# Input loads on ScalarE's DMA queue, and 27 in place of 23 activations turned by way of memory

## The chip, the cores and the metric

One core of one Trainium2 chip. The time is device microseconds of one execution, the median of the runs given. Lower is better.

## The reference

Sixteen batches of 256 tokens with 256 features (float32) go through two blocks, with 16 heads of 16 features. In the kernel's terms each batch passes three attentions and an MLP:

```
layer 0: cross attention on y, RMS norm before and after, residual (no mask in effect: all ones)
layer 1: layer norm, causal self attention with rotary positions, residual
layer 2: layer norm, cross attention on y with rotary positions, residual
MLP:     layer norm, fc1 (256 to 1024), GELU, fc2, residual
```

The output is 16 x 256 x 256 float32. Layers 1 and 2 and the MLP need the normalized activations turned, features on partitions and tokens along the row; layer 0 reads copies of x and y that the host laid out turned (`xt`, `yt`).

## The kernel before

The 48 attentions (16 batches, three layers) run one after the other in the hand-written order `ORDER = "000001010102210210210121021012210101021212122222"`, a layer's number for each place. `attended(j)` gives the batch of place j and the place (`below`) of the attention whose output it reads. The eight MLPs, on two batches each, come after the attentions. Instructions are issued in the program's order, which the code fixes by hand; engines wait for each other by semaphores.

One turn i of the main loop is attention i, in four blocks n (three for a causal one). In each block TensorE computes scores (S, L566), ScalarE their exponentials (pt, L577), GpSimd zeroes the causal half (pt, L584), and TensorE multiplies by the values (A, L605) one block later, the last part in the next attention. Between them stand parts of the neighbours:

- n = 0: `end` of attention i - 1 copies the second half of its result to memory (`hop<-av`, L623) and reads it back as sums and as `oT` (L630, L635); `pieces_in` of a turn that attention i - 1 hosted; `finish` and `divide` of earlier attentions; `q` of attention i + 1.
- n = 1: `k` of attention i + 1, and `invert` of attention i - 1, which takes the reciprocal of the sums on VectorE (L642) and sends it through memory (`inv_hop`, `inv`). For a causal attention `k` comes first, otherwise `invert`.
- n = last but one: `v` of attention i + 1, and `pieces_out` for a hosted turn.
- n = last: `project` of attention i - 2 (the output matmul and the residual; in layer 0 also the sums of squares and r_o, L246, for the norm), and a turn on TensorE if one is due.

Activations are turned in one of two ways. On TensorE, `turned` makes four 128 x 128 transposes with the identity (L286) and a copy on ScalarE (L296). By way of memory, `pieces_out` normalizes (xn, L271), transposes 32 x 32 blocks on VectorE (L306), and writes to memory (`turn_hop`, L311); `pieces_in` reads them back in four DMAs (`hT`, L317) one attention later. `turned_ahead` assigns each attention j of layers 1 and 2 a host m from j - 8 to j - 3 in which its `pieces_out` is issued, by matching with augmenting paths; those without a host are turned on TensorE in attention j - 2 (`due_turn`).

The tile of `pieces_out` has the tag "a", of which there are two buffers; `rotated` (the rotary part of q and k, L468) and `fold_bias` use the same tag. PSUM holds two pairs of banks for S and one for A.

Loads of weights and of later batches stand in a list `due`. When the attention three places ahead is of layer 0, four loads of 256 KB for its batch (`cur`, `y`, `xT`, `yT`) go to the front of the list. `load_next` takes from it and issues on SP's queue, which also carries every hop, turn and reciprocal.

Of the kernel before, what the change touches and what calls it, by code (L numbers as in the profile page):

```python
# [28 lines left out]
N_ATT = 3 * B  # L29

ORDER = [int(n) for n in "000001010102210210210121021012210101021212122222"]
# [15 lines left out]
def attended(j):  # L47

    b = ORDER[:j].count(ORDER[j])
    return b, [i for i in range(N_ATT) if ORDER[i] == ORDER[j] - 1][b] if ORDER[j] else None  # L50


def turned_ahead():


    slots = {}

    def place(j, tried):
        for m in range(j - 3, max(attended(j)[1] + 2, j - 8), -1):
            if ORDER[m] != 1 and m not in tried:  # L60
                tried.add(m)
                if m not in slots or place(slots[m], tried):
                    slots[m] = j
                    return True
        return False

    for j in range(N_ATT):
        if ORDER[j] > 0:
            place(j, set())
    return slots  # L70
# [3 lines left out]
def xattn_kernel(  # L74
# [21 lines left out]
    nc = tc.nc  # L96
# [580 lines left out]
    def att(i):  # L677
        if i is not None and 0 <= i < N_ATT:
            return atts.setdefault(i, Att(i))
        return None  # L680

    def do(i, *names):
        a = att(i)
        for name in names:
            if a is not None:
                getattr(a, name)()
# [287 lines left out]
    with tc.manual_schedule():  # L974
# [34 lines left out]
            due.append((fc2_sb[:, 2 * j : 2 * j + 2], fc2[j * D : (j + 1) * D]))  # L1009
        due = [(t, w.rearrange("(k p) n -> p k n", p=P)) for t, w in due]  # L1010

        def load_next(i, n, later):

            if not (i > 1 and ahead is not None and ahead.layer == 0):
                n = later if i > 2 else 0
            for t, w in due[:n]:
                nc.sync.dma_start(out=t, in_=w)
            del due[:n]

        turns = turned_ahead()  # L1020
        for i in range(N_ATT):
            a, last = att(i), att(i - 1)
            sent, due_turn = turns.get(i), i + 2 if i + 2 not in turns.values() else None
            fresh = sent is not None and att(sent).below == i - 3
            ahead = att(i + 3)
            if i > 1 and ahead is not None and ahead.layer == 0:
                due[:0] = batch(ahead.b)
            load_next(i, 2, 1)

            finishing = i >= 3 and att(i - 3).layer == 0
            follows = finishing and i + 2 < N_ATT and att(i + 2).below == i - 3
            for n in range(len(a.blocks)):
                if n == 0 and a.causal and not finishing:
                    do(due_turn, "stats")
                a.scores(n)
                if n > 0:
                    a.values(n - 1)
                elif last is not None:  # L1040
                    last.values(-1)
                final = len(a.blocks) - 1
                if n == 0:
                    if i == 0:
                        a.v()
                        do(1, "spread")
                    late = finishing and i + 2 < N_ATT and att(i + 2).layer == 0
                    if not follows and not late and (finishing or not a.causal):
                        do(due_turn, "stats")
                    if sent is not None and not fresh:  # L1050
                        do(sent, "stats")
                    do(i - 1, "end")
                    do(turns.get(i - 1), "pieces_in")
                    if late:
                        do(due_turn, "stats")
                    do(i - 3, "finish")
                    if follows:
                        do(due_turn, "stats")
                    if fresh:
                        do(sent, "stats")  # L1060
                    if not finishing:
                        do(due_turn, "norm")
                    if i == N_ATT - 3:
                        mlps[0].stats()
                    if i == N_ATT - 2:
                        mlps[0].norm()
                    do(i - 2, "divide")
                    if i == N_ATT - 1:
                        mlps[0].turn(nc.vector.tensor_copy)
                        mlps[0].keep()  # L1070
                    if i + 1 < N_ATT:
                        att(i + 1).q(both=not a.causal)
                elif n == 1:

                    if a.causal:
                        do(i + 1, "k", "second_mask")
                    if last is not None:
                        last.invert(lambda: do(i + 2, "send"))
                    else:
                        do(i + 2, "send")  # L1080
                    do(i + 2, "receive")
                    load_next(i, 1, 1)
                    if not a.causal:
                        do(i + 1, "k")
                    if finishing:
                        do(due_turn, "norm")
                    for j in kept.get(i, ()):
                        att(j).keep()
                    if i == N_ATT - 1:
                        do(i - 2, "project")  # L1090
                        mlps[1].norm()
                if n == final - 1:
                    do(i + 1, "v")
                    do(sent, "pieces_out")
                    if i == N_ATT - 2:
                        mlps[1].stats()
                    if i == N_ATT - 1:
                        mlps[0].up(2)
                        mlps[0].mix("hT", HT_LIVE)
                if n == final:  # L1100
                    if i == N_ATT - 1:
                        mlps[1].turn(nc.vector.tensor_copy)
                    else:
                        do(i - 2, "project")
                    do(due_turn, "turn")
                    load_next(i, 1, 0)
                if i == 0 and n == 0:
                    load(4)
                    nc.sync.dma_start(out=bias_sb, in_=rows.partition_broadcast(P))
                    nc.sync.dma_start(out=turn_sb, in_=turn)  # L1110
                if i == 0 and n == 1:
                    load_w(ca_sb, ca[:1], nc.sync)
                if i == 1 and n == 0:
                    load_w(sao_sb, [sa_o], nc.sync)
                if i == 1 and n == 2:
                    nc.sync.dma_start(
                        out=rope_sb, in_=rope.rearrange("(c p) t d -> p c t d", p=P)
                    )
                if i == 1 and n == 3:
                    att_hop = fold_bias(  # L1120
                        [(sa_sb, j * D, V_B1) for j in range(3)] + [(ca_sb, 0, V_B2)]
                    )
                if i == 2 and n == 2:
                    att_cols = fold_back(att_hop)
                    row_v = fc2_sb[:, 0]
                    nc.sync.dma_start(out=row_v, in_=att_hop[2].partition_broadcast(P))
                if i == 2 and n == 3:
                    fold_gain(sa_sb, slice(0, 3 * D), V_G1)
                if i == 3 and n == 3:
                    fold_att(att_cols, row_v)  # L1130
                if i == 8 and n == 2:
                    fold_gain(ca_sb, slice(0, D), V_G2)
                if i == 11 and n == 3:
                    fc1_hop = fold_bias([(fc1_sb, j * D, V_B3) for j in range(4)])
                if i == 12 and n == 1:
                    fc1_cols = fold_back(fc1_hop)
                if i == 14 and n == 2:
                    fold_fc1(fc1_cols)
                if i in (14, 15) and n == 1:
                    fold_gain(fc1_sb, slice(0, FF), V_G3, [i - 14], nc.gpsimd)  # L1140
                if n == 1 and i > 15 and not a.causal:
                    next(combined, None)
# [12 lines left out]
        for g in range(B // 2):  # L1155
            this = mlps[g]
            ahead, next_but_one, third = (
                mlps[i] if i < B // 2 else None for i in (g + 1, g + 2, g + 3)
            )
# [67 lines left out]
    with tc.If(n_good < P):  # L1227
        with tc.tile_pool(name="gen", bufs=1) as gen, tc.tile_pool(
# [4 lines left out]
                out=hop.rearrange("(n p) -> p n", p=P),  # L1233
                in_=qk_bias.rearrange("p n t -> p (n t)"),
# [3 lines left out]
                out=qk_row.rearrange("p n d -> p (n d)"), in_=hop.partition_broadcast(P)  # L1238
# [5 lines left out]
        with tc.tile_pool(name="late2", bufs=2) as late2, tc.tile_pool(  # L1244
# [3 lines left out]
            for g in range(B // 2):  # L1248
                m = Mlp(g, late2)
# [393 lines left out]
```

## Time and profile before

| What | us |
|---|---|
| median of 3 runs (lowest, highest) | 936.03 (930.95, 939.96) |
| profiled execution, its own time | 938.71 |
| span of the profile | 936.7 |
| TensorE busy | 918.8 |
| VectorE busy | 679.6 |
| ScalarE busy | 530.8 |
| GpSimd busy | 310.8 |
| attentions, first score matmul to last | 10.6 to 727.8 |
| mean granted clock of TensorE | 0.998 |

Engines are named PE (TensorE matmul), PEld (its weight loads), DVE (VectorE), ACT (ScalarE), POOL (GpSimd) and SP; SPq and ACTq are the DMA queues that SP and ScalarE issue to. A row of a timeline gives start, duration, engine, line, operation, what is written and read, and how many were merged; in brackets the time that the engine sat idle before it and what ended it. Times run from the span's start. The length of an attention is the time from its first score matmul to that of the next.

### The profile page before, as it was taken

How to read it: one execution, taken by the hardware profiler on the slowest of the kernel's cores; microseconds unless marked ns; L12 is line 12 of the kernel's file. 1: busy time of each engine (PE TensorE's matmuls, PEld its weight loads, DVE VectorE, ACT ScalarE, POOL GpSimd, SP SyncE). 2: the span in 40 equal slices, each digit the busy share in tenths (PEclk: the TensorE clock that was granted, in tenths of full speed). 3: DMA queues.
4: the chain of work that ended last, by engine and by line, in shares of the span. 5: the costliest groups of instructions: out<-in, count | busy, mean ns of one | idle time of the engine just before them, and what ended most of it. 6: DMA issues, size and time to landing. Idle time of an engine off the chain costs nothing.

```text
span 936.7 us, 29330 instructions
## 1 busy us (share of the span) xinstructions
PE 918.8 (98%) x12226; PEld 536.5 (57%) x12226; DVE 679.6 (73%) x1501; ACT 530.8 (57%) x744; POOL 310.8 (33%) x503
## 2 busy tenths in 40 slices
PE   8999999999999999999999899999999999999997
PEld 4444444445444554454445444555444799999997
DVE  4458667866879687868976578887877597777663
ACT  3666655655656665656656556666666634444440
POOL 4213552324353545434443242552332041111100
PEclk9999999999999999999999999999999999999999
DMA  9433444435243343433444333232322101222201
GB/s 290 158 109 119 138 149 144 142 117 146 93 135 116 109 127 112 138 121 96 139 123 143 100 116 106 84 105 85 107 79 72 58 9 61 68 69 68 70 24 48
DMA packets 122751, 100.52 MB, mean 107 GB/s; under 512 B 24298, under 2 KB 118130, under 8 KB 122610
## 3 DMA queue, kind: packets, MB, share of 16 engines
q1 hardware_dynamic: 121922, 98.02, 33.7%
q8 instruction: 98, 1.61, 0.7%
q10 hardware_dynamic: 688, 0.54, 0.2%
q14 instruction: 43, 0.35, 0.1%
HBM read 59.70 MB, written 38.82 MB: 105 GB/s over the span
## 4 chain that ended last, share of the span: by engine, by line
PE 76%; DVE 9%; DMA 8%; SPq 2%; issue 2%; POOL 2%; ACT 0%; ACTq 0%; DVEq 0%; POOLq 0%
PE S L566 15%; PE A L605 14%; PE d L364 13%; PE d L352 12%; PE upX L788 6%; PE A L886 5%; DMA hop<-av 5%; PE downZ L886 3%; PE upZ L788 3%; PE d L886 2%; PE d L788 1%; DMA sums<-hop 1%; DMA inv_hop<-sums 1%; DVE u L476 1%; POOL pt L584 1%
## 5 line engine op out<-in xcount | busy, mean ns | idle before, releaser
L577 ACT ACTIVATE pt<-S 128x1024 f32<-128x1024 f32 x224 | 217.3, 1022 | 133.8 <-PE S L566 133.8
L566 PE MATMUL S<-qm,kT 32*128 32x512 f32 (+1 forms) x1536 | 204.3, 602 | 5.8 <-DVE kT L525 4.0
L605 PE MATMUL A<-pt,va 128*32 128x256 f32 (+1 forms) x3072 | 193.0, 368 | 2.8 <-POOL pt L584 1.6
L605 PEld LDWEIGHTS A<-pt,va 128*32 128x32 f32 x3072 | 81.0, 109 | 160.5 <-issue 94.6
L577 ACT ACTIVATE pt<-S,sy 128x1024 f32<-128x1024 f32 x128 | 135.6, 1111 | 50.6 <-PE S L566 50.0
L584 POOL TENSOR_SCALAR_AFFINE_SELECT pt<-pt 128x512 f32<-128x512 f32 x128 | 89.6, 715 | 148.2 <-ACT pt L577 147.5
L566 PEld LDWEIGHTS S<-qm,kT 32*128 32x128 f32 x1536 | 62.9, 184 | 77.9 <-issue 40.1
L468 ACT ACTIVATE a<-d,qk_bias 128x256 f32<-128x256 f32 x128 | 53.6, 470 | 55.6 <-PE d L352 36.3
L340 POOL TENSOR_TENSOR cur<-cur,bias 128x512 f32<-128x512 f32 x48 | 70.9, 1482 | 31.4 <-DVE xn L271 31.4
L352 PE MATMUL d<-hT,sa 128*32 128x256 f32 x1024 | 61.2, 379 | 0.4 <-DMA hT<-turn_hop 0.4
L810 ACT COPY g<-upX 128x512 f32<-128x512 f32 x28 | 15.0, 589 | 72.4 <-issue 67.5
L246 POOL TENSOR_SCALAR r_ln<-bmv 128x2 f32<-128x2 f32 x48 | 13.5, 280 | 125.4 <-DVE bmv L265 123.8
L476 DVE TENSOR_TENSOR u<-u,turn 128x512 f32<-128x512 f32 x64 | 52.4, 818 | 0.0
L476 DVE TENSOR_TENSOR a<-a,turn 128x512 f32<-128x512 f32 x64 | 48.1, 752 | 2.2
L622 DVE COPY av<-A 128x512 f32<-128x512 f32 x47 | 32.2, 685 | 24.0 <-PE A L605 23.5
L656 DVE TENSOR_TENSOR oT<-oT,inv 128x512 f32<-128x512 f32 x48 | 38.1, 794 | 13.1 <-DMA inv<-inv_hop 5.4
L472 DVE STREAM_SHUFFLE u<-a 128x512 f32<-128x512 f32 x64 | 47.4, 740 | 0.0
L826 ACT ACTIVATE g<-g,fb 128x256 f32<-128x256 f32 x96 | 41.0, 499 | 11.1 <-DVE g L815 11.1
L246 POOL TENSOR_SCALAR r_o<-ms_o 128x2 f32<-128x2 f32 x16 | 3.9, 241 | 130.9 <-DVE sq L254 121.3
L352 PEld LDWEIGHTS d<-hT,sa 128*32 128x32 f32 x1024 | 33.5, 110 | 22.6 <-DMA hT<-turn_hop 1.3
L271 DVE TENSOR_SCALAR xn<-cur,bmv,r_ln 128x256 f32<-128x256 f32 x96 | 41.4, 480 | 0.8 <-POOL r_ln L247 0.8
L881 DVE TENSOR_TENSOR g<-g,g 128x512 f32<-128x512 f32 x64 | 40.5, 680 | 0.0
(150 smaller groups left out, 1557.1 us busy)
## 6 DMA issues: line engine op xcount, KB each, us to landing
hop<-av SPq DMA_DIRECT2D x96, 256.0 KB
oT<-hop SPq DMA_DIRECT2D x96, 128.0 KB
inv<-inv_hop SPq DMA_DIRECT2D x96, 128.0 KB
turn_hop<-turn SPq DMA_DIRECT2D x33, 256.0 KB
hT<-turn_hop SPq DMA_DIRECT2D x132, 64.0 KB
xT<-in_xt SPq DMA_DIRECT2D x16, 256.0 KB
cur<-in_x SPq DMA_DIRECT2D x16, 256.0 KB
yT<-in_yt SPq DMA_DIRECT2D x16, 256.0 KB
```

What stands on the lines that cost most here:

```text
L340: nc.gpsimd.tensor_tensor(t, t, bias_sb[:, row : row + D].unsqueeze(1).to_broadcast([P, NC, D]), ALU.add)
L352: nc.tensor.matmul(o, lhsT=w[:, k, at + t * P + j : at + t * P + j + 32], rhs=tokens, start=(k == 0), stop=(k == KC - 1), skip_group_check ...
L364: nc.tensor.matmul(ps[j : j + 32, c * D : (c + 1) * D], lhsT=some_tokens(src, k, c, j), rhs=w[:, k, at : at + D], start=(k == 0), stop=(k ...
L468: nc.scalar.activation(a[:, t], ps[:, t], AF.Identity, bias=bias[:, t : t + 1])
L472: nc.vector.stream_shuffle(u.rearrange("p t s -> p (t s)"), a.rearrange("p t s -> p (t s)"), SWAP)
L476: nc.vector.tensor_tensor(t, t, table.unsqueeze(1).to_broadcast([P, KC, S]), ALU.mult)
L566: nc.tensor.matmul(ps[:, j, 2 * m * u : 2 * m * (u + 1)] .rearrange("p (i s) -> p i s", i=2), lhsT=self.kT[r, t, kc * P : (kc + 1) * P], r ...
L577: nc.scalar.activation(pt[:, :, :w], ps[:, :, :w], AF.Exp, scale=scale)
L584: nc.gpsimd.affine_select(out=diag, in_=diag, compare_op=ALU.is_ge, fill=0.0, base=0, pattern=[[0, 2], [0, 2], [1, P]], channel_multiplier=-1,
L605: nc.tensor.matmul(self.av[32 * r : 32 * r + 32, i, q0:S], lhsT=self.va[:, kc, 8 * t + 2 * r + i, :], rhs=pts[r // 2][:, r % 2, i * m : (i ...
L788: nc.tensor.matmul(o if len(b.shape) == 2 else by_groups(o), lhsT=a[:, c * P : (c + 1) * P], rhs=b, start=(first and c % 2 == 0), stop=Tru ...
L886: nc.tensor.matmul(ps[:, c, :], lhsT=a[f // 2][:, f % 2, c * P : (c + 1) * P], rhs=b[:, f, :], start=(first and c == 0 and f == 0), stop=True,
```

## The change

Four edits, all in the order of issue; what is computed stays the same.

1. `turned_ahead` may also pick a causal attention as a host when the one after it is of layer 0. The matching then finds 27 hosts in place of 23. Hosts before: 4, 6, 8, 10, 11, 12, 15, 17, 18, 20, 22, 24, 25, 27, 29, 30, 32, 34, 36, 37, 39, 41, 43. Hosts after: 4, 6, 8, 10, 12, 13, 16, 18, 19, 20, 22, 23, 24, 25, 26, 27, 30, 31, 32, 33, 34, 35, 36, 37, 39, 41, 43. Attentions turned on TensorE: 5, 12, 18, 22, 31, 38, 43, 45, 47 before; 5, 12, 18, 45, 47 after.
2. `load_next` issues on ScalarE's queue in place of SP's.
3. It is called at four places that take one load each, where before the start of the attention took two. In an attention whose third successor is of layer 0, all four load; in the others (from i = 3 on) the first two.
4. When attention i - 2 is of layer 0, `pieces_out` is issued behind its `project`, not before it.

```diff
@@ def turned_ahead
+    hosts = [m for m in range(N_ATT - 1) if ORDER[m] != 1 or ORDER[m + 1] == 0]
...
         for m in range(j - 3, max(attended(j)[1] + 2, j - 8), -1):
-            if ORDER[m] != 1 and m not in tried:
+            if m in hosts and m not in tried:
@@ main loop
-        def load_next(i, n, later):
-            if not (i > 1 and ahead is not None and ahead.layer == 0):
-                n = later if i > 2 else 0
+        def load_next(i, later=0):
+            n = 1 if i > 1 and ahead is not None and ahead.layer == 0 else later * int(i > 2)
             for t, w in due[:n]:
-                nc.sync.dma_start(out=t, in_=w)
+                nc.scalar.dma_start(out=t, in_=w)
             del due[:n]
@@ start of attention i
-            load_next(i, 2, 1)
@@ n == 0, behind divide and ahead of q
+                    load_next(i, 1)
@@ n == 1
+                    load_next(i, 1)
                     if a.causal:
                         do(i + 1, "k", "second_mask")
...
                     do(i + 2, "receive")
-                    load_next(i, 1, 1)
                     if not a.causal:
                         do(i + 1, "k")
+                    load_next(i)
@@ n == final - 1
                     do(i + 1, "v")
-                    do(sent, "pieces_out")
+                    late_out = i > 1 and att(i - 2).layer == 0
+                    if not late_out:
+                        do(sent, "pieces_out")
@@ n == final
                         do(i - 2, "project")
+                    if late_out:
+                        do(sent, "pieces_out")
                     do(due_turn, "turn")
-                    load_next(i, 1, 0)
+                    load_next(i)
```

## The prediction

> **What bounds the kernel now.** I read the page first, then the windows of single attentions, then the timelines of the windows that were longer than others of their kind.
>
> ```profile
> PE 918.8 (98%) x12226; PEld 536.5 (57%) x12226; DVE 679.6 (73%) x1501; ACT 530.8 (57%) x744; POOL 310.8 (33%) x503
> ```
>
> TensorE bounds the span of 936.7 us (the profiled execution took 938.71, so 2.0 lie around it). The attentions fill 10.6 to 727.8, the MLPs the rest, which the change leaves alone. In TensorE's timeline I took each attention's first score matmul (S) as its start. The lengths fall on a few values: 12.70 for a causal attention, 15.19 for another, 15.63 where a causal one went before. What lies above these is a turn on TensorE or a stall. An undisturbed causal attention beside a disturbed one:
>
> ```profile
> 119.55:133.31 13.76, 13.38 (x208) 6.80 (x208) 8.94 (x20) 6.60 (x8) 6.53 (x12) 1.00 0.50 166
> 303.17:315.87 12.70, 12.70 (x213) 6.68 (x209) 5.42 (x10) 6.61 (x8) 5.12 (x10) 1.00 0.44 132
> ```
>
> Columns: length, then busy time and count of TensorE, its weight loads, VectorE, ScalarE, GpSimd; clock; DMA. TensorE counts as busy in both, so its 0.68 us more are matmuls stretched by waits. The cause, in the timelines of attention 7, VectorE's, GpSimd's and TensorE's (start, duration, engine, line; idle time before and its releaser in brackets):
>
> ```profile
> 119.92 0.73 DVE L271 TENSOR_SCALAR xn<-cur,bmv,r_ln 128x256 f32<-128x256 f32 x2
> 120.69 0.77 DVE L306 STREAM_TRANSPOSE turn<-xn 128x256 f32<-128x256 f32 x2
> 121.38 0.65 DVE L662 TENSOR_TENSOR s<-d,cur 128x512 f32<-128x512 f32 x1
> ```
>
> ```profile
> 123.06 0.22 POOL L246 TENSOR_SCALAR r_o<-ms_o 128x2 f32<-128x2 f32 x1 [11.14 <-DVE sq L254]
> 123.36 0.71 POOL L247 TENSOR_TENSOR r_o<-r_o,nhalf 128x2 f32<-128x2 f32 x1
> 124.03 1.42 POOL L584 TENSOR_SCALAR_AFFINE_SELECT pt<-pt 128x512 f32<-128x512 f32 x2
> ```
>
> ```profile
> 124.73 1.61 PE L605 MATMUL A<-pt,va 128*32 128x256 f32 x14 [0.23 <-POOL pt L584]
> ```
>
> VectorE does the hosted turn (xn, turn) before the residual (s) of a first-layer attention; GpSimd's r_o waits for that, the causal selects (pt) queue behind r_o, and the values matmul (A) waits for the selects. The second kind of stall, attention 34, in the timelines of SP, VectorE and TensorE, and the window behind it:
>
> ```profile
> 524.74 0.46 SPq L1017 DMA_DIRECT2D xT<-in_xt  x1
> 525.29 0.42 SPq L623 DMA_DIRECT2D hop<-av  x1
> 525.76 0.47 SPq L1017 DMA_DIRECT2D yT<-in_yt  x1
> 526.32 0.52 SPq L623 DMA_DIRECT2D hop<-av  x1
> 532.13 0.55 SPq L630 DMA_DIRECT2D sums<-hop  x1
> ```
>
> ```profile
> 534.39 0.35 DVE L642 RECIPROCAL sums<-sums 128x32 f32<-128x32 f32 x1 [2.86 <-DMA sums<-hop]
> ```
>
> ```profile
> 537.66 2.09 PE L566 MATMUL S<-qm,kT 32*128 32x512 f32 x8 [2.74 <-DVE kT L525]
> ```
>
> ```profile
> 537.50:540.90 3.40, 3.24 (x20) 1.14 (x24) 3.30 (x10) 1.06 (x2) 0.00 (x0) 0.50 0.52 166
> ```
>
> SP's queue sends two input loads between the hops. SP reaches the sums 5.8 us after it issued the last hop, against about 2.3 in undisturbed attentions. The reciprocal waits for the sums, the next kT stands behind it on VectorE, TensorE idles 2.74 us and then has half its clock for 3.4 us. A third, in attention 12, ScalarE's timeline and TensorE's:
>
> ```profile
> 203.64 0.84 ACT L468 ACTIVATE a<-d,qk_bias 128x256 f32<-128x256 f32 x2 [4.17 <-DMA turn_hop<-turn]
> ```
>
> ```profile
> 205.44 2.04 PE L566 MATMUL S<-qm,kT 32*128 32x512 f32 x8 [1.42 <-ACT pt L577]
> ...
> 331.50 0.66 PE L286 MATMUL d<-ident,xn 128*128 128x128 f32 x4
> ```
>
> Attention 11 hosts a turn and folds a bias, both in tiles of tag "a" (two buffers), so the rotation in 12 waits for the turn's DMA. The last line is a turn on TensorE: 331.50 to the next S at 332.08, 0.58 us.
>
> **What the Trainium skill says.** "TensorE: Matmul & The Clock Gate", Part 1, has the half clock come after an idle window of about 3.4 us; the trace gave it already after 2.74 us idle. "DMA: Bandwidth & Descriptors", Issuing engines are not separate DMA queues, says that a second issuing engine saves issue time alone, since all run on the same 16 DMA engines; its section Queues, rings and completion order has each of these take turns between the queues, by packets. The trace has ScalarE issue only at the start, so no run here shows that yet. With it, a hop is no longer behind a whole load, but still shares with it.
>
> **The change part by part.**
>
> *Four turns leave TensorE* (those for attentions 22, 31, 38 and 43; 5, 12, 18, 45 and 47 stay). 4 x 0.58 = 2.3 us, all on the path. Four copies of 0.585 leave ScalarE, off the path. VectorE gains 4 x 2 transposes of 0.40, 3.2 us, off the path where it has room: hosting moves to causal attentions, where it is busy 5 to 6 of 12.7 us.
>
> *A hosted turn goes behind the projection when attention i - 2 is of layer 0.* This is so for hosts 4, 6, 8, 12, 22 and 34, whose next attention is causal and finishes a first-layer one. There xn and turn (1.53 us) stand ahead of s; r_o at 3.51 us into attention 7 comes at about 1.98, and the two selects end at about 4.4 in place of 5.9, before the values at 4.9 ask for them. Excess over 12.70: attentions 5, 7 and 23, 1.06 each; 9, 1.59; 13, 0.71: together 5.48. Attention 16 has 0.89 of the same sort beside its turn (14.17 - 12.70 - 0.58): GpSimd takes the statistics of 18 ahead of its selects, and VectorE is late because 15 hosts; 15 no longer does. All 6.4 taken. What is late next: the copy of A (av, L622). With the turn and, where not "fresh", 1.2 us of statistics ahead of it, it ends at about 5.1 to 5.2 us in attentions 13, 23 and 37, while the values need the bank at 4.87: a loss of 0.3 each, 1.0 together; 20 and 27 are within 0.2 of it.
>
> *Attention 11 hosts no more*: the 2.39 us that 12 has over 15.19 go.
>
> *Loads leave SP's queue.* Four loads per batch of 256 KB (11 batches, at i = 3, 5, 7, 11, 14, 17, 21, 24, 29, 31, 33) and eleven weights: each gives SP back about 0.47 us and stands no longer ahead of a hop. Attentions 34 and 35 lose their 3.31 + 1.51 (the second is the half clock), 6 and 8 their 1.17 + 0.85 (hops that landed at 11 us rather than at 5), 22 its 0.25: 7.1 us. Bounds: all 7.1, or nothing if the loads slow the hops all the same.
>
> *Loads enter ScalarE's queue*, about 0.5 us each (its two weight loads at the start took 0.50 and 0.52 to issue). Three of the four places fall where ScalarE is idle anyway (before q, at the start of block 1, at the end). The third, after the copies of k, does not: behind it are the exponentials of block 2, then the copy of A. By the built program's order this load waits there, in 11, 14, 17 and 24, for the first oT<-hop of the same attention. In attention 24 that was issued at 6.8 us and landed at 9.9 by the trace's semaphore counts, while k's copies end at 9.01 and the exponentials start at 9.27. With the issue they start at about 10.45; they may be 0.9 to 1.0 us late before TensorE waits for a bank. So about 0.3 each, 1.2 together. Below nothing it can't be; above, with the landing at 12.9 as in attention 11 of now, 3.2 each. In the causal 5, 7, 31 and 33 block 2 starts later (exponentials from 10.5 at the earliest): nothing.
>
> *Sum against the profiled execution*: 938.7 - 2.3 - 6.4 - 2.4 - 7.1 + 1.0 + 1.2 = 922.7. The median before is 2.7 lower than that execution; its runs spread over 9 us, and I take the stall of 34 (4.8) for something that some have and others not. From the median, with half of that stall: 936.0 - 2.3 - 6.4 - 2.4 - 2.3 - 2.4 + 2.2 = 922.4. I say 923.
>
> **Rivals.**
>
> *The stalls move* (0.25). The same 16 DMA engines carry loads, hops and four more turns (each 256 KB out and back); hosts now follow each other in 30 to 37, and SP then issues seven DMAs between a hop and the reciprocal's. For: 34's stall began in such a crowd. Against: without loads SP's work per attention is some 7.5 us of issuing. Then the 7.1 stay, or their like: 923 + 7.1, about 930.
>
> *The turn behind the projection only shifts the wait* (0.10): VectorE does the same work, av comes late in all eleven late hosts' successors by 0.5, and half of the 6.4 returns: 923 + 5 + 3, about 931.
>
> *ScalarE held by the waits for oT* (0.12), the case on the slower side. One mechanism: the third load of a batch, in order on ScalarE, waits for SP's chain. It decides from a landing at 9.9; each us later in 11, 14, 17 and 24 is a us of TensorE. If the chain lags as in attention 34 of now, where the sums were issued at 13.4 and oT landed at 17, or half as far (14.0), each loses 4.1, and two such pauses bring the half clock at 1.5: 923 + 16.4 + 3 = 942. For: nothing releases ScalarE earlier. Against: the chain is late in before mainly because of the loads that now leave it.
>
> **How the numbers follow.** Forecast 0.53, rivals 0.25, 0.10 and 0.12. 1% (9.4 us, about what a measurement of this kernel can tell from no change) puts the border at 926.7. The forecast's own range is 917 to 929, so four fifths of it are faster by over 1%, and a third of each of the first two: 0.43 + 0.12, and some for execution-to-execution stalls that I counted half: 0.58. Slower by over 1% only in the third, 0.11. Range 915 to 936: it takes in the first two rivals and leaves out the third.
>
> **What would show it.** Right: 5, 7, 9, 13 and 23 at 12.7 to 13.0; 12 at 15.2; 34 at 15.6 and no half clock; TensorE's busy time about 9 us down; ScalarE's first exponential of block 2 in 11, 14, 17, 24 at about 10.5 us. Wrong: these at 12 or more with TensorE idle behind pt; waits of S for kT elsewhere; A waiting for av.

## The result, and the profile after

| | before | after |
|---|---|---|
| median of the runs taken side by side, us | 933.91 (22 runs) | 937.0 (22 runs) |
| ratio after/before, 95% interval | | 1.0022 (1.0006 to 1.0038) |
| profiled execution, its own time, us | 938.71 | 936.99 |
| span of the profile, us | 936.7 | 935.2 |
| attentions, first S to last S, us | 10.6 to 727.8 | 10.5 to 726.1 |
| mean granted clock of TensorE | 0.998 | 0.993 |

The ratio is estimated from the runs side by side and isn't the quotient of the two medians. The change makes the kernel 0.2% slower, with an interval just clear of 1, where 923.0 us (915 to 936) was forecast. Most of what the prediction took for gains is there in the profile; one cost that it put at 1.2 us has eaten them.

First the lines that answer to those shown of before. The page's line of busy times:

```profile
PE 920.8 (98%) x12210; PEld 537.5 (57%) x12210; DVE 682.3 (73%) x1509; ACT 528.7 (57%) x740; POOL 310.8 (33%) x503
```

TensorE runs 16 instructions fewer (four turns of four transposes) and is still 2.0 us longer busy: matmuls have become longer. Not in the causal attentions that the change was to mend. The window of attention 7, then VectorE's, GpSimd's and TensorE's timelines in it:

```profile
118.72:131.43 12.71, 12.71 (x213) 6.68 (x209) 8.14 (x19) 6.61 (x8) 6.11 (x12) 1.00 0.63 184
```

```profile
118.86 0.69 DVE L663 TENSOR_TENSOR s<-d,cur 128x512 f32<-128x512 f32 x1 [0.92 <-PE d L365]
119.59 0.42 DVE L255 SCALAR_TENSOR_TENSOR sq<-s 128x256 f32<-128x256 f32 x1
...
120.41 0.73 DVE L272 TENSOR_SCALAR xn<-cur,bmv,r_ln 128x256 f32<-128x256 f32 x2
```

```profile
120.58 0.32 POOL L247 TENSOR_SCALAR r_o<-ms_o 128x2 f32<-128x2 f32 x1 [7.66 <-DVE sq L255]
120.98 0.73 POOL L248 TENSOR_TENSOR r_o<-r_o,nhalf 128x2 f32<-128x2 f32 x1
121.67 1.23 POOL L585 TENSOR_SCALAR_AFFINE_SELECT pt<-pt 128x512 f32<-128x512 f32 x2
```

```profile
123.60 1.07 PE L606 MATMUL A<-pt,va 128*32 128x256 f32 x16
```

The residual (s) now stands ahead of the hosted turn (xn), r_o comes 1.86 us into the attention, the selects end at 4.2 and the values (A) start at 4.9 without a wait: 12.71 us in place of 13.76. The crowd in attention 34 has thinned too, in SP's timeline and TensorE's:

```profile
523.92 0.41 SPq L312 DMA_DIRECT2D turn_hop<-turn  x1
524.42 1.98 SPq L624 DMA_DIRECT2D hop<-av  x2
529.02 0.55 SPq L631 DMA_DIRECT2D sums<-hop  x1
```

```profile
538.05 1.14 PE L567 MATMUL S<-qm,kT 32*128 32x512 f32 x8
```

SP reaches the sums 7.5 us into the attention (13.4 before), and the next S starts with no idle time and at the full clock. Attention 34 takes 16.53 us and 35 takes 12.70, together 3.9 less.

Now what is new. In the waits of TensorE and of ScalarE (engine, line and what it waited for: us in total, times, longest) one line each stands out. The first was 1.7 us before, the second wasn't there:

```profile
PE S L567 <- ACT pt L578: 4.7, 4, 2.2
```

```profile
ACT pt L578 <- DMA oT<-hop: 14.7, 4, 3.9
```

The exponentials (pt) don't read oT. They stand in ScalarE's queue behind a load whose issue waits for it. The windows of attentions 14 and 24, 15.63 us each before:

```profile
220.83:241.09 20.26, 18.33 (x245) 8.06 (x241) 9.31 (x18) 10.92 (x14) 4.97 (x5) 0.92 0.51 151
371.03:393.22 22.19, 20.00 (x244) 8.72 (x240) 11.62 (x25) 10.92 (x14) 4.29 (x7) 0.85 0.51 157
```

They are 4.6 and 6.6 us longer, with granted clocks of 0.92 and 0.85. Attention 24, in the timelines of SP, ScalarE and TensorE:

```profile
372.41 1.23 SPq L651 DMA_DIRECT2D inv<-inv_hop  x2
373.74 0.41 SPq L312 DMA_DIRECT2D turn_hop<-turn  x1
374.25 0.92 SPq L624 DMA_DIRECT2D hop<-av  x2
379.76 0.55 SPq L631 DMA_DIRECT2D sums<-hop  x1
380.36 1.21 SPq L636 DMA_DIRECT2D oT<-hop  x2
```

```profile
379.58 0.47 ACT L469 ACTIVATE a<-d,qk_bias 128x256 f32<-128x256 f32 x1
383.47 0.39 ACTq L1017 DMA_DIRECT2D xT<-in_xt  x1
383.96 2.12 ACT L578 ACTIVATE pt<-S,sy 128x1024 f32<-128x1024 f32 x2 [3.92 <-DMA oT<-hop]
```

```profile
385.13 3.08 PE L567 MATMUL S<-qm,kT 32*128 32x512 f32 x8 [2.19 <-ACT pt L578]
```

k's copy (a, L469) ends at 9.0 us into the attention. The third load of the batch (xT) is next on ScalarE and goes out at 12.43, just after the first oT landed (12.41 by the trace's semaphore counts). The exponentials follow at 12.9, after 3.9 us in which ScalarE did nothing; TensorE runs out of free banks, idles 2.19 us, and has then half its clock. The window behind the pause:

```profile
386.10:392.90 6.80, 6.80 (x54) 2.67 (x52) 0.98 (x3) 2.58 (x3) 0.00 (x0) 0.50 0.50 156
```

Attention 14 is alike: 1.93 us idle, then 3.41 us at half clock. So 24's 6.56 us are 2.19 idle, 3.4 of lost clock (half of 6.8) and a rest of 1.0, which I take for matmuls stretched before and after; 14's 4.62 are 1.93, 1.7 and 1.0.

### The profile page after: what moved, and what is told of

The parts are those of the page before. It is cut to its first block, busy times and chain, and to the rows that moved or that the text cites. A ratio compares the mean times of both kernels' runs of the same rounds, so it can differ in the third digit from the quotient of the medians.

```text
span 935.2 us, 29335 instructions
## 1 busy us (share of the span) xinstructions
PE 920.8 (98%) x12210; PEld 537.5 (57%) x12210; DVE 682.3 (73%) x1509; ACT 528.7 (57%) x740; POOL 310.8 (33%) x503
## 4 chain that ended last, share of the span: by engine, by line
PE 86%; DVE 6%; DMA 4%; issue 1%; ACT 1%; POOL 0%; SPq 0%; ACTq 0%; DVEq 0%
PE S L567 18%; PE A L606 16%; PE d L365 15%; PE d L353 15%; PE upX L789 6%; PE A L887 5%; PE downZ L887 3%; PE upZ L789 3%; PE d L887 2%; PE d L789 1%; DMA oT<-hop 1%; ACT pt L578 1%; DVE u L477 1%; DVE a L477 1%; DVE u L473 1%
## 5 line engine op out<-in xcount | busy, mean ns | idle before, releaser
L567 PE MATMUL S<-qm,kT 32*128 32x512 f32 (+1 forms) x1536 | 209.4, 602 | 5.6 <-ACT pt L578 4.7
L606 PE MATMUL A<-pt,va 128*32 128x256 f32 (+1 forms) x3072 | 190.4, 369 | 0.4 <-DVE av L623 0.3
L585 POOL TENSOR_SCALAR_AFFINE_SELECT pt<-pt 128x512 f32<-128x512 f32 x128 | 87.1, 695 | 143.2 <-ACT pt L578 142.2
L469 ACT ACTIVATE a<-d,qk_bias 128x256 f32<-128x256 f32 x128 | 53.6, 470 | 53.5 <-PE d L353 38.3
L247 POOL TENSOR_SCALAR r_ln<-bmv 128x2 f32<-128x2 f32 x48 | 15.7, 327 | 130.9 <-DVE bmv L266 129.9
L477 DVE TENSOR_TENSOR u<-u,turn 128x512 f32<-128x512 f32 x64 | 55.6, 869 | 0.0
L666 DVE TENSOR_TENSOR cur<-d,cur 128x512 f32<-128x512 f32 x32 | 21.7, 677 | 35.1 <-PE d L365 34.8
L657 DVE TENSOR_TENSOR oT<-oT,inv 128x512 f32<-128x512 f32 x48 | 35.6, 742 | 15.2 <-DMA inv<-inv_hop 11.8
```

The costliest lines, as they stand in the source:

```text
L469: nc.scalar.activation(a[:, t], ps[:, t], AF.Identity, bias=bias[:, t : t + 1])
L477: nc.vector.tensor_tensor(t, t, table.unsqueeze(1).to_broadcast([P, KC, S]), ALU.mult)
L567: nc.tensor.matmul(ps[:, j, 2 * m * u : 2 * m * (u + 1)] .rearrange("p (i s) -> p i s", i=2), lhsT=self.kT[r, t, kc * P : (kc + 1) * P], r ...
L585: nc.gpsimd.affine_select(out=diag, in_=diag, compare_op=ALU.is_ge, fill=0.0, base=0, pattern=[[0, 2], [0, 2], [1, P]], channel_multiplier=-1,
L606: nc.tensor.matmul(self.av[32 * r : 32 * r + 32, i, q0:S], lhsT=self.va[:, kc, 8 * t + 2 * r + i, :], rhs=pts[r // 2][:, r % 2, i * m : (i ...
```

## The experiments

Each median is compared with that of the kernel before run beside it, since the latter moved between 931.97 and 933.91. In the expectations theory A is that the third load's wait for oT holds ScalarE; theory B, that the loads slow the hops because all share the DMA engines, and the crowd of turns does the rest. xT is the third load.

### The third load, and it alone

*The third load back on SP's queue, the other three on ScalarE's.*

```diff
-        def load_next(i, later=0):
+        def load_next(i, later=0, eng=nc.scalar):
...
-                nc.scalar.dma_start(out=t, in_=w)
+                eng.dma_start(out=t, in_=w)
@@ n == 1, behind the copies of k
-                    load_next(i)
+                    load_next(i, eng=nc.sync)
```

> The changed kernel with the third load of a batch (xT, behind the copies of k) issued on SP's queue at the same place of the program; the other three places stay on ScalarE. Theory A (ScalarE held by the wait for oT): the waits of ScalarE for oT<-hop, 14.7 us in the changed kernel, go, attentions 14 and 24 return from 20.25 and 22.19 to about 15.7 and the half clocks with them; about 14 us less than the changed kernel, 921 to 925 us. Theory B (the loads slow the hops because all share the DMA engines, and the crowd of turns does the rest): about as the changed kernel, 933 to 938.

*The third load on ScalarE's queue, but at the end of the attention, ahead of the fourth.*

```diff
@@ n == 1, behind the copies of k
-                    load_next(i)
@@ n == final
                     do(due_turn, "turn")
+                    load_next(i)
                     load_next(i)
```

> The changed kernel with the third load moved, still on ScalarE's queue, to the end of the attention, directly ahead of the fourth. Theory A: as with the third load on SP, 920 to 925 us, and the nearest to what the prediction summed up (923). Theory B: as the changed kernel, 933 to 938.

Measured: 922.08 and 921.47 us beside 931.97, ratios 0.990 (0.988 to 0.9919) and 0.9891 (0.9872 to 0.9911). Eleven 256 KB loads, moved to the other queue or to a later place, are worth over 1%. The second has the lowest median of all, below both kernels. Its page, its windows of the same two attentions (14 and 24) and ScalarE's timeline in 24:

```profile
PE 910.1 (99%) x12210; PEld 534.4 (58%) x12210; DVE 681.8 (74%) x1509; ACT 529.0 (57%) x740; POOL 309.4 (34%) x503
```

```profile
218.60:234.23 15.63, 15.63 (x245) 7.52 (x241) 9.36 (x18) 10.91 (x14) 4.97 (x5) 1.00 0.48 143
363.54:379.17 15.63, 15.63 (x244) 7.51 (x241) 11.64 (x25) 10.92 (x14) 4.29 (x7) 1.00 0.46 147
```

```profile
371.71 0.84 ACT L469 ACTIVATE a<-d,qk_bias 128x256 f32<-128x256 f32 x2 [0.56 <-PE d L353]
372.81 2.12 ACT L578 ACTIVATE pt<-S,sy 128x1024 f32<-128x1024 f32 x2 [0.26 <-PE S L567]
```

The oT of 24 lands here at 12.0 us, hardly earlier than in the changed kernel (with the load on SP at 13.0, later). Nobody on ScalarE waits for it, the exponentials start 9.3 us into the attention, and nothing is lost. (At its new place the load waits too, in 24 until 13.8 us for a piece of a turn, with nothing urgent behind it.) So the late chain of hops costs nothing by itself in these two attentions; the cost is the instruction that waits for it in front of the exponentials. Attention by attention, the changed kernel's excess over this one is 4.62 (14), 6.56 (24), 0.74 (11), 0.68 (17), 1.17 (5 and 6), 1.05 (33 and 34), with -0.25 in others (attention 0, at the start, left out): 14.6 us. The profiled executions differ by 15.0, the medians, each against the kernel before beside it, by 13.6 (+3.1 and -10.5).

*A transfer of 4 bytes at the third place, all else as in the version above.* It keeps the wait and takes away the bytes.

```diff
@@ load_next
+        probe = dram.tile([1, 1], F32, tag="probe", name="probe", bufs=1)
@@ n == 1, behind the copies of k
+                    if i > 1 and ahead is not None and ahead.layer == 0:
+                        nc.scalar.dma_start(out=probe, in_=vec[0:1, 0:1])
```

> The kernel with xT moved to the end (921.5 us), and at the third place of each batch a DMA of four bytes on ScalarE's queue, from a constant to memory. In the built program it waits for the first oT<-hop in attentions 11, 14, 17 and 24, as xT did there in the changed kernel. If the wait alone is the price (theory A): ScalarE is held as in the changed kernel, 932 to 938 us. If the 256 KB at that moment are the price: 921 to 924 us.

Measured: 935.58 beside 933.54, ratio 1.0025 (1.0003 to 1.0047). The 4 bytes cost about as much as the load, in the same places: 14 (19.92 us), 24 (22.68) and 17 (16.82). The waits of ScalarE and its timeline in 14:

```profile
ACT pt L578 <- DMA oT<-hop: 18.2, 6, 4.8
```

```profile
233.88 0.25 ACTq L1087 DMA_DIRECT2D probe<-vec  x1
234.24 2.12 ACT L578 ACTIVATE pt<-S,sy 128x1024 f32<-128x1024 f32 x2 [3.31 <-DMA oT<-hop]
```

The 256 KB are not the cause, then, nor can the issue be, at 0.25 us here and 0.37 there, against waits of 3.0 us on average (18.2 in 6). The wait itself comes from the order of the program: in the built program the DMAs share eight counters in turn, and an issue waits for the DMA that used its counter last. For the third load that is the first oT of the same attention in 5, 7, 11, 14, 17, 24, 31 and 33. The trace of the changed kernel bears it out: in all eight the load uses the counter of that oT, and goes out 0.02 us after it landed.

### Which part of the change makes the wait long

*The changed kernel with the 23 old hosts, and the kernel before with the loads alone changed.* Both are shown against the changed kernel.

```diff
@@ the first: turned_ahead
-            if m in hosts and m not in tried:
+            if ORDER[m] != 1 and m not in tried:
@@ the second: the same, and in the main loop
-                    late_out = i > 1 and att(i - 2).layer == 0
+                    late_out = False
```

> The changed kernel with the 23 hosts of before; loads on ScalarE at the four places and the turn behind the projection stay. With these hosts the third load of attentions 14, 17, 24 and 29 waits in the built program for the batch's own first load, which has long landed, and only 11 waits for oT. Theory A: no pause of ScalarE in 14 and 24, four turns more on TensorE (2.3 us): 924 to 928 us. Theory B (crowd of turns and loads): faster than the changed kernel as well, but then ScalarE's wait for oT would have to stay, or be without effect.

> The kernel before with only its loads changed (ScalarE's queue, four places); hosts and the place of pieces_out as before. By the prediction's terms: the late hops of 6, 8, 22, 34 and 35 go (up to 7.1 us in the profiled execution before, about 4 from the median) and the stalls of the causal attentions 5, 7, 9, 13, 23 (5.5) and of 12 (2.4) stay: 929 to 932 us, against 934 before. If loads on a second queue slow the hops as much as in SP's: 933 to 936.

Measured: 929.47 and 928.67 beside 931.97, ratios 0.9972 (0.9958 to 0.9985) and 0.997 (0.9952 to 0.9988). Attentions 14 and 24 are back at 15.63 in both, although oT lands at 11.2 and 12.4 in the first. The hosts shift the counting: with the old 23 the third load in 14, 17 and 24 waits for its own batch's `cur`, which was issued long before. Where it still waits for oT, it can still cost; the expectation had only 11 wait so, but by the counters 5, 7, 31 and 33 do too, and the first kernel missed its 924 to 928. ScalarE's waits in it have

```profile
ACT pt L578 <- DMA oT<-hop: 6.5, 2, 4.3
```

and attentions 31 and 32 take 13.94 and 16.53 us in both kernels (12.70 and 15.63 in the second with its third load last, below). What a load at the third place costs thus hangs on how many DMAs happen to be issued before it.

*The changed kernel with `pieces_out` always ahead of the projection.*

```diff
-                    late_out = i > 1 and att(i - 2).layer == 0
+                    late_out = False
```

> The changed kernel with pieces_out ahead of the projection again; xT stays at the third place, where it waits for oT in 11, 14, 17 and 24 as in the changed kernel. With xT at the end, oT landed at 11.3 (attention 14) and 12.0 (24) with the turn behind the projection, and at 10.9 and 10.2 with it ahead. If the late oT comes from the turn behind the projection: attention 24 loses its pause and the half clock (6.5 us), 14 keeps part of its 4.6: 925 to 931 us. If it comes from the loads on ScalarE's queue: as the changed kernel, 933 to 938.

Measured: 931.01 beside 932.52, ratio 0.9981 (0.9963 to 0.9998); 937.0 had been 1.0022. The wait stays, but is shorter, in the waits of ScalarE:

```profile
ACT pt L578 <- DMA oT<-hop: 9.4, 3, 3.5
```

Attention 24 falls from 22.19 to 16.58, 14 only to 19.12. The first oT lands in 24 at 10.1 us, in place of 12.4. SP's timeline in 24, which starts here at 370.33:

```profile
369.97 1.23 SPq L651 DMA_DIRECT2D inv<-inv_hop  x2
371.30 0.40 SPq L312 DMA_DIRECT2D turn_hop<-turn  x1
376.72 0.55 SPq L631 DMA_DIRECT2D sums<-hop  x1
```

The turn of 23, a host only since the change, stands ahead of both hops with either order (compare the lines of 24 above); 13 and 23 are not among the hosts whose turn is late. What moves is the whole queue: with the turns of 12 and 22 late, the reads of the reciprocal (`inv`) that stand ahead of it go out at 1.4 us into attention 24 in place of -0.4, and SP reaches the sums at 8.7 in place of 6.4 (6.2 in the kernel before). The four kernels with loads on ScalarE at all four places part the two edits. In 24 the first oT lands at 10.0 us with neither, 10.1 with the new hosts, 12.4 with the late turn and 12.4 with both: the late turn alone makes it late. In 14 it lands at 10.3, 11.0, 11.2 and 12.2: both add. The new hosts also put that oT in front of the third load. So the hosts, the late turn and the third load meet in the same two attentions.

### What the parts are worth without that wait

*Loads alone, third load last; then the 27 hosts as well; then the turn behind the projection only where the next attention is causal.* The first is against the kernel before, the others against the best version.

```diff
@@ first: the kernel before, with the changed load_next, all loads on ScalarE, no load behind k
                     do(due_turn, "turn")
-                    load_next(i, 1, 0)
+                    load_next(i)
+                    load_next(i)
@@ second
-                    late_out = i > 1 and att(i - 2).layer == 0
+                    late_out = False
@@ third
-                    late_out = i > 1 and att(i - 2).layer == 0
+                    late_out = i > 1 and att(i - 2).layer == 0 and ORDER[i + 1] == 1
```

> The kernel before with only its loads changed, and xT at the end of the attention. Against the loads alone at the four places (928.7 us) the waits for oT in 11 and 31 go (0.5 and about 2.1 with what follows in 32): 925 to 927 us. If ScalarE's waits for the loads had no part there: 928 to 930 us.

> The kernel with xT moved to the end (921.5 us), with pieces_out ahead of the projection again in every attention. The prediction gave this order 6.4 us (the causal attentions 5, 7, 9, 13, 16 and 23): 928 us. But with the loads alone changed, 7, 9 and 13 were already at 12.7 to 12.9, and 5 and 23 alone kept 1.0 each: if the late hops were the larger cause, 923 to 925 us.

> The kernel with xT moved to the end (921.5 us), with the turn behind the projection only where the next attention is causal (hosts 4, 6, 8, 12, 22, 34), ahead of it in 10, 16, 19, 26 and 36. Attention 38's stall (0.65 us, with the turn of 36 behind the projection) goes if that turn is its cause, the causal ones keep their gain: 920.5 to 921.5 us.

Measured: 926.99 and 923.93 beside 933.54, and 923.72 beside 932.52; ratios 0.9925 (0.9901 to 0.9949), 0.989 (0.9868 to 0.9911) and 0.9908 (0.9888 to 0.9927). The loads are worth 6.5 us, the hosts another 3.1, and the place of the turn nothing that can be told: the second and third and the best version have overlapping intervals, and spans of 920.4, 920.5 and 920.2. By attentions the late turn gains 1.07 in 5 and 0.80 in 23 and gives back 1.23 in 6, 13, 32 and 38. That it should be 36's late turn that costs 38 its 0.65 us was a guess, and the third kernel, expected at 920.5 to 921.5, refutes it: there 36's turn is ahead, and 38 still takes 13.36. Its trace has TensorE idle for 0.59 us before the next S, waiting for kT, and VectorE behind from the product with `inv` on: `inv` came at 4.9 us into the attention (4.4 in the second kernel). What makes it late there stays open.

*The late turn alone and the 27 hosts alone, in the kernel before.*

```diff
@@ first: the kernel before, with the turn late
+                    late_out = i > 1 and att(i - 2).layer == 0
+                    if not late_out:
                         do(sent, "pieces_out")
...
+                    if late_out:
+                        do(sent, "pieces_out")
                     do(due_turn, "turn")
@@ second: the kernel before, with 27 hosts
-            if ORDER[m] != 1 and m not in tried:
+            if (ORDER[m] != 1 or m < N_ATT - 1 and ORDER[m + 1] == 0) and m not in tried:
```

> The kernel before with only the hosted turn put behind the projection where attention i - 2 is of layer 0; loads in SP's queue and hosts as before. By the prediction's term for the causal attentions: 5.5 us less than before (932 to 934), 927 to 929 us. If the late hops are what makes VectorE late there: within 2 us of before.

> The kernel before with only the 27 hosts; loads in SP's queue and pieces_out as before. Four turns leave TensorE (2.3 us). With the loads repaired the step from 23 to 27 hosts was worth 3.1 us (927.0 to 923.9). Without it the crowd of turns meets the late hops: 930 to 934 us; above 935 if the added turns make the hops later still.

Measured: 935.32 beside 933.54 and 935.2 beside 932.52, ratios 1.0013 (0.9992 to 1.0033) and 1.0021 (0.9999 to 1.0042). Alone, neither brings a gain. The late turn mends the causal attentions (5, 7, 13 and 23: 12.70; 9: 12.80) but 6 and 8 grow to 17.90 and 18.18; with the new hosts 34 takes 19.87. The stalls move, which is what the prediction's first rival said, though of the kernel with all edits.

*The changed kernel with all its loads on SP's queue, at the new four places.*

```diff
-                nc.scalar.dma_start(out=t, in_=w)
+                nc.sync.dma_start(out=t, in_=w)
```

> The changed kernel with all loads issued on SP's queue, at the four places of the changed kernel. ScalarE then waits for no load (theory A: none of its 14.7 us), but the loads stand between SP's hops again, behind the first hop and no longer ahead of it. If leaving the start of the attention is what helps, and not the queue: 921 to 925 us. If SP's queue is what makes the hops late: 927 to 934 us.

Measured: 931.97 beside 932.52, ratio 0.9987 (0.9967 to 1.0006). 14 and 24 are whole (15.63 and 15.78), but 8, 25 and 34 take 18.30, 17.61 and 20.46. Attention 34 starts at 512.34 us; SP's timeline and TensorE's:

```profile
519.07 0.45 SPq L1017 DMA_DIRECT2D xT<-in_xt  x1
519.62 0.41 SPq L312 DMA_DIRECT2D turn_hop<-turn  x1
520.13 0.38 SPq L624 DMA_DIRECT2D hop<-av  x1
520.56 0.53 SPq L1017 DMA_DIRECT2D yT<-in_yt  x1
521.18 1.12 SPq L624 DMA_DIRECT2D hop<-av  x1
527.31 0.56 SPq L631 DMA_DIRECT2D sums<-hop  x1
```

```profile
532.79 1.24 PE L567 MATMUL S<-qm,kT 32*128 32x512 f32 x4 [2.40 <-DVE kT L526]
```

It is the stall of the kernel before, with the last hop issued at 8.9 us and landed at 14.9, and the sums behind it. So the loads have to leave SP's queue for the rest to pay in full. "DMA: Bandwidth & Descriptors", section Issuing engines are not separate DMA queues, has a second issuing engine save issue time alone. Here the same loads at the same places give 931.97 us on SP and 937.0 on ScalarE; with the third at the end on ScalarE, 921.47. With issues of about 0.4 us each, far more than their issue time hangs on which in-order queue they stand in, and where in it.

## Why the prediction was wrong, point by point

**The step that failed** is *Loads enter ScalarE's queue*, the term of +1.2 us in the sum (0.3 each in 11, 14, 17 and 24, and nothing in the causal attentions). It measured 14.6. The mechanism was named, and so was its sign (exponentials of block 2 at 12 us or more, with TensorE idle behind pt): it is there in 14 and 24. Its rule nearly holds, too: the load waits for the first oT, and what exceeds some 0.95 us of slack is lost. With the landings of the changed kernel the rule gives 2.5 and 2.7 for 14 and 24, where 2.9 and 3.2 were lost apart from the clock; in 11 and 17 it gives nothing and 0.2, where 0.74 and 0.68 were lost. What was mis-sized went into it:

- The landing. 9.9 us was that of attention 24 of the kernel before, taken for all four. Its trace has 11.5 in 14, 9.7 in 17 and 12.9 in 11; with these the same rule gives about 5 us in place of 1.2. The first oT came at 12.2, 9.9 and 9.7 in 14, 17 and 11, and at 12.4 in 24. The prediction expected the chain of hops to come earlier without the loads; it did not ask what its other edits do to that chain. The late turn moves the landing in 24 from 10.0 to 12.4, and in 14 it and the new hosts add 1.9 together.
- The half clock. It takes 5.1 us of the 14.6. The prediction held it back for a rival with landings at 14.0; the one pause with half clock that it had seen was 2.74 us long.
- The causal attentions. "Nothing" was 2.2: in 33 the first oT landed at 11.2 us, the exponentials of block 2 waited 3.4 us for it, and 34 lost 0.90.

The rival *ScalarE held by the waits for oT* is what came true, in two attentions of its four; its 942 was built on 4.1 lost in each.

**Four turns leave TensorE**, -2.3: right. 20, 29, 36 and 41 go from 16.22 to 15.63 (20 to 15.75).

**The turn behind the projection**, -6.4: the lengths came as foretold (12.70 to 13.11 for the five), but the term was credited with what another edit earns as well. The order alone mends all five. But with the loads alone 7, 9 and 13 are at 12.87, 12.70 and 12.70, their turn still ahead of s: the loads in SP's queue had a part in it there, and either edit is enough. The order is needed in 5 and 23, 1.9 us; the 0.89 of 16 needs the new hosts, without regard to the order.

**Attention 12**, -2.4: it is at 15.19, but also with the loads alone, where 11 hosts as ever. Either edit is enough, so the two terms were not separate. The windows of 7 and 12 with the loads alone:

```profile
117.63:130.50 12.87, 12.87 (x212) 7.07 (x209) 8.19 (x18) 6.61 (x8) 6.18 (x12) 1.00 0.61 189
191.58:206.77 15.19, 15.19 (x228) 7.08 (x224) 13.65 (x33) 10.29 (x14) 5.83 (x10) 1.00 0.39 118
```

**Loads leave SP's queue**, -7.1: right in kind and too small. With the third load last, the loads alone take the profiled execution from 938.7 to 926.2, in 34 and 35, 6 and 8, and in what was credited to the order in 7, 9 and 13 and to the host in 12. (Of the two loads that the prediction saw between the hops of 34, its lines have one between them and one ahead of both.)

**Late copies of A**, +1.0: at most half. 23 is 0.36 over and waits 0.29 for av; 13 is 0.16 over without such a wait; 37 shows none.

**The sum.** With the third load last the profiled execution is 922.0, where the same sum without its 1.2 gives 921.5. That is partly luck: the order was credited with more than it was needed for and the loads with less, and each stall was counted once. From median to median that version gains 10.5 rather than 16.7, since the profiled execution of before was among its long ones (938.71, in runs of 929.11 to 939.96); the allowance made for that in the prediction was right in sign.

## What to carry to other kernels

A DMA issued by ScalarE stood in its queue like any other instruction: 14.7 us of exponentials waited behind it for a transfer that they don't read. Before placing one on a compute engine, find what its issue waits for in the built program, and put it where nothing urgent stands behind it. That wait depends on how many DMAs are issued before it, so an edit elsewhere (here four more turns) can turn a harmless place into a costly one. A wait that an edit adds is sized from the latest landing in each of its places, with all edits of the change in effect, and not from the one place where it looks best.

## What the runs showed of the hardware

- The half clock came after 1.93 and 2.19 us of idle TensorE, for 3.41 and about 6.8 us. "TensorE: Matmul & The Clock Gate", Part 1, has an idle window of about 3.4 us; the measurement decides. But the length of the pause alone does not settle it. With all loads on SP's queue a pause as long, in attention 25, brought none; in the changed kernel with `pieces_out` ahead, 0.74 us in attention 14 was enough, where the eight score matmuls behind the pause took 2.13 us in place of 1.14. The lines of the first, then of the second:

```profile
399.40 1.14 PE L567 MATMUL S<-qm,kT 32*128 32x512 f32 x8 [1.93 <-DVE kT L526]
399.40:402.80 3.40, 3.40 (x52) 1.77 (x56) 3.37 (x8) 1.94 (x2) 0.81 (x2) 1.00 0.29 100
```

```profile
232.97 2.13 PE L567 MATMUL S<-qm,kT 32*128 32x512 f32 x8 [0.74 <-ACT pt L578]
235.30:238.70 3.40, 3.40 (x40) 1.73 (x35) 0.00 (x0) 1.12 (x2) 0.00 (x0) 0.50 0.54 165
```

- The stretches at half clock lie on a grid. In the changed kernel the trace's clock records have them start at 235.96, 386.14 and, at the kernel's end, 932.27 us, which is 44.0 and 160.0 times 3.413 us apart. So where a pause falls in such a step may count as well as its length; that is an inference from these starts. In the changed kernel the half clock added 1.7 us to the pause of 1.93 and 3.4 to that of 2.19.
- Issuing a load on ScalarE took 0.37 to 0.42 us in mid-kernel in the changed kernel, and can overlap an exponential that is already running: `cur` goes out at 1.35 us into attention 24, while the first exponentials run. With the third load last, 14 and 24 hold four such issues each and keep their 15.63 us.
- A DMA of 4 bytes cost about what one of 256 KB cost (935.58 us, ratio 1.0025, and 937.0, ratio 1.0022), since the wait ahead of it is the price.
